# A gated recurrence over 512 steps: 24 sums of weights moved from GpSimd to VectorE

## The chip, the cores and the metric

The kernel runs on one core of one Trainium2 chip. The time is device time in microseconds. A core has five engines that run their own instruction queues in order and meet at semaphores: TensorE (PE; its weight loads are shown apart as PEld), VectorE (DVE), ScalarE (ACT), GpSimd (POOL) and SyncE (SP), which here only issues transfers between HBM and SBUF, the on-chip memory. Matmuls write to a second on-chip memory, PSUM.

## The reference

x is (8, 512, 512): 8 sequences, 512 steps, 512 features. One gated recurrent layer runs over the steps and its states are added to x:

```python
def step(h, x_t):
    fused = sigmoid(concatenate([x_t, h], -1) @ w_W + w_b)
    r, z = split(fused, 2, -1)
    m = x_t @ wx_W + wx_b + r * (h @ wh_W + wh_b)
    h_new = z * h + (1 - z) * tanh(m)
    return h_new, h_new
_, hs = scan(step, h0, swapaxes(x, 0, 1))
return x + swapaxes(hs, 0, 1)
```

All products with x_t (512 by 1536 weights) can be taken for many steps at once. The products with h (again 512 by 1536) can't: each step needs the state of the step before.

## The kernel before, in words

*Layout.* The 512 units stand in four blocks `k` of 128 partitions. A matmul takes 32 columns of the state or of x (4 steps of 8 sequences) as its stationary operand and writes 32 rows of PSUM. The steps are handled in groups of 4, and in chunks of `TC` = 16 steps, for which x is loaded and the output stored.

*One step of the recurrence.* TensorE takes the state's products in an order written out by hand (`ORDER`): A0 to A3 (parts of all gates, one for each block k), D0 to D3, and of H only the last two blocks. All of them are issued through the helper at L203. Behind them, in the same queue, stand a few matmuls of the x side, named xp by their output. VectorE then works in one chain: transposes of PSUM to the layout of the scans (tr and tz at L523, md1A at L538, md1B at L580), scans (L511) that give m, ScalarE's sigmoid and tanh in between (L243), and scans that give the new state hT. The state has two halves of two blocks each, and the second half (hd0B) comes last. A0 of the next step waits for the first scan of hT and A3 for the last.

*The end of a step.* Behind the last scan VectorE has `turn_x` (L282, a transpose for a later group), in some steps `drain` (L403), in steps 0 to 3 a quarter of `weight_sum(3)` (L296), and two memsets of one column (L654). Then comes the first transpose of the next step, tr, which waits for A on TensorE. GpSimd has at the end of each step the sum of x and the state, ot (L675), and behind it the list `jobs[i]` of the step.

*The x side.* The x products of the first two chunks are taken directly: `prefill`, 4 matmuls of 384 columns at a time. Each of them shows as two records, so one `take` shows as 8 records of xp. Step 0 takes 1, steps 1 and 2 three each, step 3 two, and steps 4 to 13 one or two each by `PLAIN`. From chunk 2 on, they go through a recursive scheme with fewer products in two levels (7 products in place of 8 at each level): `products` issues 3 or 4 small blocks a step from step 14 on, `x_sum` and `inner_x` form sums of x on GpSimd (so at L330, si at L349), `drain` collects on VectorE and `result` on GpSimd.

*The sums of weights.* The scheme needs sums of the weights wx, once. The outer level has four, `weight_sum` (tw, L296), on VectorE: three ahead of step 0 and the fourth in quarters in steps 0 to 3. The inner level has 24 instructions, `inner_weight(n, p)` (ti, L315): sum n of 4, for the part p of 6. Part 0 is 768 elements on each of 128 partitions, the others 384. Parts 0 and 2 read wx, parts 3 to 6 read tw 0 to 3. Sum 1 reads sum 0, and sum 3 reads sum 1. Before the change all 24 are on GpSimd: four ahead of step 0, three a step in steps 0 to 2, two in step 3, and one a step after that until step 12. The first product that reads ti is issued in step 16.

*What sets the order.* `tc.manual_schedule()` is on: every engine runs its instructions in the order in which the program issues them.

Of the kernel before, what the change touches and what calls it, by code (L numbers as in the profile page):

```python
# [10 lines left out]
ALU = mybir.AluOpType  # L11
# [43 lines left out]
def tile_cond_rnn_residual(  # L55
# [39 lines left out]
    nc = tc.nc  # L95
# [86 lines left out]
    ti = const.tile([P, 7, 4, NQ, BL], F32, name="ti")  # L182
# [101 lines left out]
    def wx_of(kh, nh):  # L284
        return wx[:, 2 * kh : 2 * kh + 2, :, HALF * nh : HALF * nh + HALF]

    def weight_sum(n, k=slice(0, 2), j=slice(0, NQ)):

        a, b = [
            (wx_of(0, 1), wx_of(0, 0)),  # L290
            (wx_of(1, 1), tw[:, 0]),
            (wx_of(1, 1), wx_of(0, 1)),
            (wx_of(1, 0), tw[:, 1]),
        ][n]
        at = (slice(0, P), k, j)
        nc.vector.tensor_tensor(tw[:, n][at], a[at], b[at], ALU.subtract)  # L296

    def inner_weight(n, p):

        def w(k, b):  # L300
            c0 = slice(BL * b, BL * b + BL)
            if p == 0:
                return wx[:, k::2, :, c0]
            if p == 2:
                return wx[:, 2 + k, :, HALF + BL * b : HALF + BL * b + BL]
            return tw[:, p - 3, k, :, c0]

        at = slice(0, 2) if p == 0 else p
        a, b = [
            (w(0, 1), w(0, 0)),  # L310
            (w(1, 1), ti[:, at, 0]),
            (w(1, 1), w(0, 1)),
            (w(1, 0), ti[:, at, 1]),
        ][n]
        nc.gpsimd.tensor_tensor(ti[:, at, n], a, b, ALU.subtract)  # L315

    def x_block(c, r, kh):

# [119 lines left out]
    for e in range(NQ):  # L438
        turn_x(0, e)
    weight_sum(1)  # L440
    for n in (0, 2):
        for p in (0, 2):
            inner_weight(n, p)

    jobs = {}

    def at_step(i, *todo):
        jobs.setdefault(i, []).extend(todo)

    early = [(1, 0), (1, 2)] + [(n, p) for n in (0, 2, 1) for p in (3, 4, 5)]  # L450
    for n, w in enumerate(early):
        at_step(n // 3, (inner_weight, *w))
    for n, w in enumerate([(0, 6), (1, 6), (2, 6), (3, 3), (3, 4), (3, 5), (3, 6), (3, 0), (3, 2)]):
        at_step(4 + n, (inner_weight, *w))
    drains = {}
    for c in range(2, NCH):
        w0 = TC * c - LEAD
# [3 lines left out]
        for w in range(TC):  # L461
            n = done
# [10 lines left out]
    for i in range(T):  # L473
# [176 lines left out]
            seed(5)  # L650
        if i < 4:
            weight_sum(3, *[slice(v, v + 1) if w == 0 else slice(2 * v, 2 * v + 2) for w, v in enumerate(divmod(i, 2))])
        for n in range(IDLE - 3):
            nc.vector.memset(idle[:, n : n + 1], 0.0)  # L654
        def add(hf, engine):
# [105 lines left out]
```

## Time and profile before

| | |
|---|---|
| median of 3 runs | 1645.9 us (1644.61 to 1647.66) |
| the profiled execution | 1646.05 us, span of its trace 1644.0 us |
| PE busy | 1628.2 us, 99% |
| DVE busy | 1379.4 us, 84% |
| ACT busy | 976.8 us, 59% |
| POOL busy | 569.3 us, 35% |
| TensorE clock granted | 1.0 |

Each row of a timeline gives the start in microseconds from the span's beginning, the duration, the engine, the line, the operation, what is written and read, and in brackets the idle time before it with what ended it. Several equal instructions in a row are merged ("x32"). A matmul's duration includes its way through the array, so that rows of TensorE overlap; the distance between two starts is what TensorE spends on the first. The chain that ended last is followed back from the end of the program, at each instruction to what released it.

### The profile page before, as it was taken

The page shows a single profiled execution, that of the slowest core. Times are in us where ns is not written, and L with a number is a line of the kernel's source. Part 1 is how long each engine was busy: PE and PEld are TensorE (multiplying, and loading weights), DVE is VectorE, ACT ScalarE, POOL GpSimd, SP SyncE. Part 2 cuts the span into 40 slices and gives each one's busy share as a digit, 9 for nine tenths or more (in the row PEclk, how much of TensorE's full clock was granted, in tenths as well). Part 3 has the DMA queues.
Part 4 walks back from the last instruction along what each step waited for, and adds up shares of the span by engine and source line. Part 5 has one row for each costly group of instructions (what it writes and reads, how often), then busy time and mean ns, then how long its engine had stood idle before and what let it go on. Part 6 is the DMA issues. An engine that isn't in the chain of part 4 may idle for free.

```text
span 1644.0 us, 124813 instructions
## 1 busy us (share of the span) xinstructions
PE 1628.2 (99%) x53006; PEld 1360.1 (83%) x53006; DVE 1379.4 (84%) x11215; ACT 976.8 (59%) x5520; POOL 569.3 (35%) x1467
## 2 busy tenths in 40 slices
PE   8999999999999999999999999999999999999998
PEld 4788888888888888888888888888888888888876
DVE  8688888888888888888888888888888888888886
ACT  3666656556555656666656656655655566666665
POOL 7433333333333333333333333333333333333220
PEclk9999999999999999999999999999999999999999
DMA  4000000000000000000000000000000000000000
GB/s 181 11 10 18 18 18 17 6 18 17 18 18 5 18 18 18 18 17 5 18 18 18 18 5 18 18 18 17 18 5 18 18 18 18 5 18 11 12 11 10
DMA packets 11512, 31.08 MB, mean 19 GB/s; under 512 B 1220, under 2 KB 1732, under 8 KB 10952
## 3 DMA queue, kind: packets, MB, share of 16 engines
q1 hardware_dynamic: 10800, 22.94, 4.1%
q8 instruction: 414, 6.78, 1.7%
q14 instruction: 146, 1.20, 0.2%
q10 hardware_dynamic: 152, 0.16, 0.0%
HBM read 14.70 MB, written 8.39 MB: 14 GB/s over the span
## 4 chain that ended last, share of the span: by engine, by line
PE 97%; DVE 2%; POOL 1%; DMA 0%; issue 0%; ACT 0%; DVEq 0%; POOLq 0%
PE A L203 48%; PE D L203 26%; PE xp L203 16%; PE H L203 7%; DVE tr L523 0%; DVE m L511 0%; POOL ti L315 0%; DMA rows<-in_bias_dram 0%; DVE hT L511 0%; POOL xs L225 0%; DVE md1B L580 0%; DVE md1A L538 0%; DVE tz L523 0%; POOL off L229 0%; DVE tw L296 0%
## 5 line engine op out<-in xcount | busy, mean ns | idle before, releaser
L203 PE MATMUL A<-wa,hT 128*32 128x256 f32 x16352 | 885.9, 356 | 5.7 <-DVE hT L511 5.2
L203 PEld LDWEIGHTS A<-wa,hT 128*32 128x32 f32 x16352 | 507.7, 123 | 241.4 <-DVE hT L511 138.9
L203 PE MATMUL D<-wd,hT 128*32 128x128 f32 x16384 | 543.1, 273 | 1.0 <-DMA wd<-in_wd_dram 1.0
L203 PEld LDWEIGHTS D<-wd,hT 128*32 128x32 f32 x16384 | 482.8, 122 | 21.7 <-DMA wd<-in_wd_dram 1.3
L675 POOL TENSOR_TENSOR ot<-xin,hT 128x32 f32<-128x32 f32 x503 | 132.3, 263 | 1047.3 <-DVE hT L511 1035.9
L243 ACT ACTIVATE hT<-m 128x8 f32<-128x8 f32 x2048 | 324.4, 207 | 98.0 <-DVE m L511 97.7
L243 ACT ACTIVATE md0A<-tr 128x16 f32<-128x16 f32 x512 | 112.9, 220 | 407.3 <-DVE tr L523 407.3
L523 DVE STREAM_TRANSPOSE tr<-A 128x64 f32<-128x64 f32 x511 | 127.7, 250 | 229.1 <-PE A L203 229.1
L243 ACT ACTIVATE hT<-hT 128x16 f32<-128x16 f32 x1024 | 233.1, 228 | 85.0 <-DVE hT L511 84.2
L203 PE MATMUL H<-wa,hT 128*32 128x64 f32 x8208 | 210.3, 219 | 0.0
L203 PEld LDWEIGHTS H<-wa,hT 128*32 128x32 f32 x8208 | 187.5, 122 | 0.0
L511 DVE TENSOR_TENSOR_SCAN hT<-hd0A,hT 128x24 f32<-128x24 f32 x1024 | 176.3, 172 | 0.0
L511 DVE TENSOR_TENSOR_SCAN hT<-hd0B,hT 128x24 f32<-128x24 f32 x1024 | 154.4, 192 | 21.8
L511 DVE TENSOR_TENSOR_SCAN m<-md0B,md1B 128x24 f32<-128x24 f32 x1024 | 154.5, 192 | 0.0
L203 PE MATMUL xp<-ti,si 128*32 128x96 f32 x5040 | 150.1, 246 | 0.2 <-issue 0.2
L511 DVE TENSOR_TENSOR_SCAN m<-md0A,md1A 128x16 f32<-128x16 f32 x1024 | 144.2, 182 | 5.1
L243 ACT ACTIVATE md0B<-tr 128x16 f32<-128x16 f32 x512 | 116.2, 227 | 42.2 <-DVE tr L523 0.5
L418 POOL TENSOR_TENSOR xs<-ff 128x192 f32<-128x192 f32 x240 | 140.6, 596 | 0.2
L580 DVE STREAM_TRANSPOSE md1B<-A 128x64 f32<-128x64 f32 x511 | 130.0, 254 | 0.0
L243 ACT ACTIVATE hd0A<-tz 128x16 f32<-128x16 f32 x512 | 116.6, 228 | 21.4
L538 DVE STREAM_TRANSPOSE md1B<-H 128x64 f32<-128x64 f32 x512 | 127.8, 250 | 0.0
L573 DVE STREAM_TRANSPOSE hd0B<-sz 128x64 f32<-128x64 f32 x512 | 126.4, 247 | 0.0
(103 smaller groups left out, 1924.4 us busy)
## 6 DMA issues: line engine op xcount, KB each, us to landing
xin<-in_x_dram SPq DMA_DIRECT2D x31, 256.0 KB, 3.3
out_dram<-ot SPq DMA_DIRECT2D x31, 256.0 KB, 2.2
wx<-in_wx_dram SPq DMA_DIRECT2D x4, 768.0 KB, 7.1
wa<-in_wa_dram SPq DMA_DIRECT2D x4, 512.0 KB, 9.7
wd<-in_wd_dram SPq DMA_DIRECT2D x1, 768.0 KB
wd<-in_wd_dram SPq DMA_DIRECT2D x1, 256.0 KB, 11.2
out_dram<-ot SPq DMA_DIRECT2D x1, 192.0 KB, 1.8
head<-in_xh_dram ACTq DMA_DIRECT2D x1, 144.0 KB, 5.1
```

The source lines that it names most:

```text
L203: nc.tensor.matmul(out_, lhsT, rhs, start=start, stop=False, skip_group_check=True)
L243: inst = nc.scalar.activation(out_, in_, func, **kw).ins
L418: nc.gpsimd.tensor_tensor(to, a, b, ALU.add)
L511: return nc.vector.tensor_tensor_scan(*[t_[:, :, c_].rearrange("p n c s -> p (n c s)") for t_ in (out_, d0, d1)], 0.0, ALU.mult, ALU.add,).ins
L523: inst = nc.vector.transpose(t_.rearrange("p c n -> p (c n)"), raw[n][hf]).ins
L538: inst = nc.vector.transpose(md1[hf][g % 2][:, :, :, hf].rearrange("p n c -> p c n"), raw["h"][hf]).ins
L573: inst = nc.vector.transpose(hd0[1][i % 2][:, :, :, 2].rearrange("p n c -> p c n"), sz).ins
L580: nc.vector.transpose(md1[1][g % 2][:, :, :, 0].rearrange("p n c -> p c n"), ps["A"][:, :HU])
L675: pool_done[i + 1] = nc.gpsimd.tensor_tensor(ot[:, t], x_of(c, slice(0, NQ), t, 1), hTs[(i + 1) % NH][:, :, :, B * s1 : B * s1 + B, 2].rea ...
```

## The change

`inner_weight` issues its subtraction on VectorE in place of GpSimd. Of the 24, sum 0 of the parts 0 and 2 stay ahead of step 0. The other 22 are listed in `late` and issued at the ends of steps 0 to 13, behind `weight_sum` and ahead of the two memsets: two digits are n and p, and "|" divides the steps. `late` is no part of `jobs`, so these sums stand in VectorE's queue ahead of the first transpose of the next step.

```diff
-        nc.gpsimd.tensor_tensor(ti[:, at, n], a, b, ALU.subtract)
+        nc.vector.tensor_tensor(ti[:, at, n], a, b, ALU.subtract)
...
     weight_sum(1)
-    for n in (0, 2):
-        for p in (0, 2):
-            inner_weight(n, p)
-
-    jobs = {}
+    for p in (0, 2):
+        inner_weight(0, p)
+
+    jobs, late = {}, {}
...
-    early = [(1, 0), (1, 2)] + [(n, p) for n in (0, 2, 1) for p in (3, 4, 5)]
-    for n, w in enumerate(early):
-        at_step(n // 3, (inner_weight, *w))
-    for n, w in enumerate([(0, 6), (1, 6), (2, 6), (3, 3), (3, 4), (3, 5), (3, 6), (3, 0), (3, 2)]):
-        at_step(4 + n, (inner_weight, *w))
+    for n, w in enumerate("03 04|05|23|24|25 13|14 15|06 26|16|10|12 22|20|30|32 33|34 35 36".split("|")):
+        late[n] = [tuple(map(int, v)) for v in w.split()]
...
             weight_sum(3, *[slice(v, v + 1) if w == 0 else slice(2 * v, 2 * v + 2) for w, v in enumerate(divmod(i, 2))])
+        for w in late.get(i, ()):
+            inner_weight(*w)
         for n in range(IDLE - 3):
             nc.vector.memset(idle[:, n : n + 1], 0.0)
```

## The prediction

> **What bounds the kernel now.** I read the page first, then the chain that ended last, cut to 15 to 40 us, and then the timelines of TensorE, VectorE and GpSimd up to 110 us.
>
> ```profile
> span 1644.0 us, 124813 instructions
> ...
> PE 1628.2 (99%) x53006; PEld 1360.1 (83%) x53006; DVE 1379.4 (84%) x11215; ACT 976.8 (59%) x5520; POOL 569.3 (35%) x1467
> ```
>
> A busy share of 99% says little where all stages are averaged. The change touches only the first 14 of 512 steps, so the timeline of TensorE over those steps is the view that counts. Columns: start, duration, engine, line, operation, and what ended the idle time before.
>
> ```profile
> 18.10 1.10 PE L203 MATMUL D<-wd,hT 128*32 128x128 f32 x32 [0.97 <-DMA wd<-in_wd_dram]
> 19.01 0.63 PE L203 MATMUL H<-wa,hT 128*32 128x64 f32 x32
> 19.46 0.83 PE L203 MATMUL xp<-wx,head 128*32 128x384 f32 x8
> ...
> 28.48 1.06 PE L203 MATMUL D<-wd,hT 128*32 128x128 f32 x32
> ...
> 33.03 1.06 PE L203 MATMUL D<-wd,hT 128*32 128x128 f32 x32
> ...
> 37.38 1.06 PE L203 MATMUL D<-wd,hT 128*32 128x128 f32 x32
> ...
> 41.27 1.06 PE L203 MATMUL D<-wd,hT 128*32 128x128 f32 x32
> 42.15 0.41 PE L203 MATMUL H<-wa,hT 128*32 128x64 f32 x16
> 42.37 0.83 PE L203 MATMUL xp<-wx,xin 128*32 128x384 f32 x8
> 43.02 1.70 PE L203 MATMUL A<-wa,hT 128*32 128x256 f32 x32
> 44.53 1.06 PE L203 MATMUL D<-wd,hT 128*32 128x128 f32 x32
> ...
> 66.64 1.06 PE L203 MATMUL D<-wd,hT 128*32 128x128 f32 x32
> ...
> 70.11 1.06 PE L203 MATMUL D<-wd,hT 128*32 128x128 f32 x32
> ...
> 74.01 1.06 PE L203 MATMUL D<-wd,hT 128*32 128x128 f32 x32
> ...
> 77.14 1.06 PE L203 MATMUL D<-wd,hT 128*32 128x128 f32 x32
> ```
>
> The rows D are one to a step, so I use their starts as the clock; D(i) is that of step i, D(0) at 18.10. From 41.27 to 44.53 (steps 5 and 6) TensorE starts each block when the one before has been issued: D 0.88, H 0.22, xp 0.65 for 8 records, A 1.51, together 3.26. So a step with 8 records of xp takes 3.25, one with 16 takes 3.90 (37.38 to 41.27, step 4), one with 24 takes 4.55 (28.48 to 33.03, step 2). These are TensorE's own times, which no other engine's relief can shorten. Three places are longer: up to 28.48; step 3 with 16 records (33.03 to 37.38, 4.35 in place of 3.90, 0.45 lost); step 12 with 8 records (66.64 to 70.11, 3.47 in place of 3.25, 0.22 lost). From step 14 on (74.01 to 77.14) a step takes 3.13, and this goes on to the end.
>
> What is lost in the first two places is told by the chain, and by VectorE's rows.
>
> ```profile
> 15.99 5.55 POOL ti L315 x4
> 22.15 0.20 DVE hT L511
> ...
> 22.99 0.22 DVE md1A L282
> 23.21 1.69 DVE tw L296
> ...
> 35.20 0.80 DVE hT L511
> 36.06 1.50 PE A L203 x24
> ```
>
> ```profile
> 13.48 1.71 DVE L296 TENSOR_TENSOR tw<-wx,tw 128x1536 f32<-128x1536 f32 x1
> 17.18 0.25 DVE L523 STREAM_TRANSPOSE tr<-xp 128x64 f32<-128x64 f32 x1 [1.99 <-PE xp L203]
> ...
> 17.71 1.10 DVE L511 TENSOR_TENSOR_SCAN m<-md0A,md1A 128x16 f32<-128x16 f32 x2
> 19.26 0.25 DVE L523 STREAM_TRANSPOSE tr<-D 128x64 f32<-128x64 f32 x1 [0.45 <-PE D L203]
> 19.43 1.20 DVE L511 TENSOR_TENSOR_SCAN hT<-hd0A,hT 128x24 f32<-128x24 f32 x1
> ...
> 20.70 0.90 DVE L511 TENSOR_TENSOR_SCAN hT<-hd0A,hT 128x24 f32<-128x24 f32 x1
> ...
> 36.76 0.52 DVE L296 TENSOR_TENSOR tw<-wx,tw 128x384 f32<-128x384 f32 x1
> ...
> 48.68 0.25 DVE L523 STREAM_TRANSPOSE tr<-A 128x64 f32<-128x64 f32 x1 [1.10 <-PE A L203]
> ...
> 49.56 0.24 DVE L523 STREAM_TRANSPOSE tr<-D 128x64 f32<-128x64 f32 x1
> 49.73 0.17 DVE L511 TENSOR_TENSOR_SCAN hT<-hd0A,hT 128x24 f32<-128x24 f32 x1
> ...
> 50.73 0.18 DVE L511 TENSOR_TENSOR_SCAN hT<-hd0B,hT 128x24 f32<-128x24 f32 x1
> ...
> 51.94 0.25 DVE L523 STREAM_TRANSPOSE tr<-A 128x64 f32<-128x64 f32 x1 [0.90 <-PE A L203]
> ```
>
> The scan that takes 0.17 at 49.73 takes 1.20 and 0.90 in step 0, while POOL's four sums of L315 run, and 0.80 in step 3; a tw of 384 takes 0.52 at 36.76, and 1.69 in the chain for the same size at 23.21. VectorE's two-input work and POOL's sums exclude each other here, an instruction at a time. Rows of POOL show it from the other side, and what POOL keeps:
>
> ```profile
> 36.81 0.59 POOL L675 TENSOR_TENSOR ot<-head,hT 128x32 f32<-128x32 f32 x1 [0.87 <-DVE hT L511]
> ...
> 45.13 0.47 POOL L330 TENSOR_TENSOR so<-xin 128x128 f32<-128x128 f32 x1
> ...
> 47.53 0.26 POOL L675 TENSOR_TENSOR ot<-head,hT 128x32 f32<-128x32 f32 x1 [1.51 <-DVE hT L511]
> ```
>
> The ot row takes 0.26 alone and 0.59 beside the tw of 36.76.
>
> **The change, part by part.** *Removed from POOL:* all its sums of L315, four ahead of step 0 (5.55) and the rest behind the ot of each step. POOL ends no step, so this alone is worth only what it stops holding up.
>
> *Step 0.* VectorE's tr of D still starts at 19.26, since D waits for a load until 18.10. In the undisturbed step 7 the last scan of hT starts 1.17 behind that transpose (49.56 to 50.73). H of step 0 has 32 records in place of 16, which puts it 0.22 later, so the last scan starts at about 20.65, not 22.15. TensorE then has work without a gap: H, xp of 8 records (19.46), A of step 1 at 20.11; its last quarter, which needs that scan, at 20.11 + 3/4 x 1.51 = 21.24. D(1) comes at 18.10 + 0.91 + 0.45 + 0.65 + 1.51 = 21.62.
>
> *Step 1.* VectorE has, behind the scan, 0.84 of waiting for ScalarE's copy (22.15 to 22.99), then tw and the two new sums of 384 (numbers 03 and 04). I price a sum of 384 at 0.52, the tw row of the same size, and one of 768 at 0.92, on the line between 0.52 and the 1.71 of 1536. That gives 20.65 + 0.84 + 0.22 (the chain's md1A) + 3 x 0.52 = 23.3 for the next tr. This is 1.4 later than TensorE could serve it, but the first scan of hT starts 1.05 behind tr (48.68 to 49.73) and the last ends 2.23 behind it (50.73 + 0.18), at 24.5 and 25.5. A(2) starts behind 24 records, at 21.62 + 4.55 - 1.51 = 24.66, and its last quarter, which reads the last scan's part, at 25.8. TensorE just misses waiting: D(2) = 26.17, not 28.48, **2.31 gained**. If the tr were 0.5 later, 0.2 to 0.3 of that would go.
>
> *Two sums ahead of step 0* (768 and 384, 1.44) fall into the 1.99 for which VectorE waits before 17.18. Were that cover gone, step 0 still has the 0.45 idle before 19.26 and the disturbed scans' 0.9 ahead of it.
>
> *Steps 1 to 13.* VectorE needs 2.36 of a step of its own (51.94 - 48.68 - 0.90). In steps 1 to 3 come tw and one sum: 3.40 against 4.55, 4.55, 3.90. Steps 4, 6, 9 have two sums: 3.40 against 3.90; steps 8 and 11 one of 768: 3.28 against 3.90. Steps 5 and 12 have two sums and step 10 one of 768: 3.40 and 3.28 against 3.25, up to 0.15 late, but each is followed by a step of 16 records, in which the scans have 3.90 - 3.13 = 0.77 to spare. So **0.45** (step 3) and **0.22** (step 12) come back. Step 13 has three sums: 2.36 + 1.56 = 3.92 against 3.90, and if POOL's ot of 0.26 gets in between, 4.18; behind it comes a step of 3.13 without room, so **0.2 is lost** there (between 0 and 0.3).
>
> *Waits and queues.* The sums wait for nothing that comes late, and stand ahead of the next step's first transpose in VectorE's queue, which is counted above. What waits for ti is TensorE at step 16, three steps behind the last sum. No DMA moves. TensorE will want the second half of x's first chunk at 22.7:
>
> ```profile
> 9.42 4.62 SPq L119 DMA_DIRECT2D xin<-in_x_dram  x4
> ...
> xin<-in_x_dram SPq DMA_DIRECT2D x1, 128.0 KB, 9.7
> ```
>
> It lands at 9.42 + 9.7 = 19.1, in time. POOL's ot and its so and si jobs (0.26 to 0.47) now start at the end of the same step and meet the new sums. Between the bounds, a sum of 384 costs from 0.52 (nothing in the way) to 0.52 + 0.47 = 0.99 (one POOL job ahead of each); below 0.52 no row goes. I take 0.52, since the ot of 36.81 was the one that waited, not tw. The Trainium skill, page "SBUF — State Buffer", section "Who interferes with whom", says that a VectorE instruction with two SBUF inputs contends with a GpSimd one that reads SBUF, that whoever issues first holds the pair for the whole instruction, and that the other fully blocks. By that rule alone POOL's jobs hold up the new sums as often as they are held up, and the sum would be that of the first rival below; the stretched rows above agree with the lock itself, and no row of before shows two sums in a row with POOL between.
>
> *Sum.* 2.31 + 0.45 + 0.22 - 0.2 = 2.8. The profiled execution took 1646.05, so it would take 1643.25; the median of the runs shown is 1645.9, 0.15 less, so I predict **1643.1**, 0.17% less.
>
> **The rivals.** *Slower: VectorE becomes the bound of steps 1 to 13.* TensorE's time for them is 2 x 4.55 + 7 x 3.90 + 4 x 3.25 = 49.4. VectorE's is 13 x 2.36 + 3 x 0.52 + 23 d, where d is the cost of a sum of 384 and 768 counts twice: 32.3 + 23 d. At 0.52 that is 44.2. It passes TensorE's at d = 0.74 and eats the whole gain of 2.98 at d = 0.87. With the upper bound 0.99 it is 55.0, 5.6 lost, 1646.05 - 2.98 + 5.6 = 1648.7, on the median 1648.5. For it: the lock shown above, and POOL jobs in steps 4 to 11. Against it: steps 1 to 3, 12 and 13 have only the ot. Chance 0.1, half of it beyond 0.2%.
>
> *Only the late stalls go.* If step 0 is held by something that stands behind POOL's sums and that no row shows, the last scan stays near 22.15, tw falls from 1.69 to 0.52 and the two sums take 1.04 of that back: D(2) gains 0.1, the others 0.67, less 0.2: 0.6, 1645.3. Against it: VectorE's scans in step 0 have no idle time before them that something else ended. Chance 0.1.
>
> *The other 498 steps shift.* Nothing of the change runs there, but 0.01 in each is 5 us, either way: 1638 or 1648. Chance 0.03 each.
>
> **How the numbers follow.** About 0.2%, 3.3 us, is what a measurement of this kernel can tell from no change; the three runs lie 3.05 apart. My case has 0.74. Its 2.8 lies 0.5 below that bound, so the measured difference may well pass it: 0.36 faster, 0.38 within. Its own range is 1642.0 to 1644.5. With the late-stall case the range is 1641.9 to 1645.5; outside remain most of the slower rival, the shifts and the edges of my own case, 2 in 10. Faster 0.36 + 0.03 = 0.39; slower 0.05 + 0.03 = 0.08, which I set to 0.10 for a collision priced too low; same 0.51.
>
> **What would show it.** Right: scans of step 0 at 0.2 and no L315 on POOL; D(2) near 26.2, D(4) near 34.6, D(14) near 71.2; steps of 3.13 afterwards. Wrong: rows of L315 on VectorE well above 0.52, idle time of VectorE before tr gone with TensorE waiting for hT in steps 4 to 13, or D(1) still near 23.

## The result and the profile after

The changed kernel takes 1643.83 us (median of 18 runs, 1641.65 to 1645.41), the kernel before 1646.83 beside it (18 runs, 1644.61 to 1649.39): ratio 0.9979, 95% interval 0.9972 to 0.9986, so faster by 0.21%, or 3.0 us between the medians. The prediction said 2.8 us less, 1643.1; that figure started from 1645.9, and the kernel before came out 0.9 higher in these runs, so the differences are what compares.

TensorE's timeline after the change, with the rows D as the clock of the steps, as in the prediction:

```profile
17.92 1.11 PE L203 MATMUL D<-wd,hT 128*32 128x128 f32 x32 [0.96 <-DMA wd<-in_wd_dram]
18.84 0.63 PE L203 MATMUL H<-wa,hT 128*32 128x64 f32 x32
19.29 0.83 PE L203 MATMUL xp<-wx,head 128*32 128x384 f32 x8
19.93 1.70 PE L203 MATMUL A<-wa,hT 128*32 128x256 f32 x32
21.45 1.06 PE L203 MATMUL D<-wd,hT 128*32 128x128 f32 x32
...
25.99 1.06 PE L203 MATMUL D<-wd,hT 128*32 128x128 f32 x32
...
34.44 1.06 PE L203 MATMUL D<-wd,hT 128*32 128x128 f32 x32
...
66.96 1.06 PE L203 MATMUL D<-wd,hT 128*32 128x128 f32 x32
...
70.86 1.06 PE L203 MATMUL D<-wd,hT 128*32 128x128 f32 x32
...
73.99 1.05 PE L203 MATMUL D<-wd,hT 128*32 128x128 f32 x32
```

From D(0), which still waits for its load, to D(14) there is no idle time on TensorE any more. Counted from each kernel's own D(0), so that a load that lands 0.18 earlier doesn't count, D(14) comes at 70.86 - 17.92 = 52.94 in place of 74.01 - 18.10 = 55.91: 2.97 us less, in the stage where the change is. Then a step takes 3.13, as before.

VectorE in the same stretch:

```profile
14.99 1.68 DVE L315 TENSOR_TENSOR ti<-wx 128x768 f32<-128x768 f32 x2
17.02 0.25 DVE L519 STREAM_TRANSPOSE tr<-xp 128x64 f32<-128x64 f32 x1 [0.35 <-PE xp L203]
...
17.55 0.28 DVE L507 TENSOR_TENSOR_SCAN m<-md0A,md1A 128x16 f32<-128x16 f32 x2
19.09 0.25 DVE L519 STREAM_TRANSPOSE tr<-D 128x64 f32<-128x64 f32 x1 [1.26 <-PE D L203]
19.27 0.17 DVE L507 TENSOR_TENSOR_SCAN hT<-hd0A,hT 128x24 f32<-128x24 f32 x1
...
20.56 0.18 DVE L507 TENSOR_TENSOR_SCAN hT<-hd0B,hT 128x24 f32<-128x24 f32 x1
...
21.55 0.51 DVE L296 TENSOR_TENSOR tw<-wx,tw 128x384 f32<-128x384 f32 x1
21.98 1.02 DVE L315 TENSOR_TENSOR ti<-tw 128x384 f32<-128x384 f32 x2
22.93 0.24 DVE L519 STREAM_TRANSPOSE tr<-A 128x64 f32<-128x64 f32 x1
...
37.02 0.51 DVE L315 TENSOR_TENSOR ti<-tw 128x384 f32<-128x384 f32 x1
37.46 0.62 DVE L315 TENSOR_TENSOR ti<-tw,ti 128x384 f32<-128x384 f32 x1
...
69.47 1.52 DVE L315 TENSOR_TENSOR ti<-tw,ti 128x384 f32<-128x384 f32 x3
...
71.11 0.25 DVE L519 STREAM_TRANSPOSE tr<-A 128x64 f32<-128x64 f32 x1
```

The scans of step 0 are at 0.17 where they had 1.20 and 0.90; the last one of the state starts at 20.56 in place of 22.15. The tw at the end of step 0 takes 0.51, not 1.77. Sums of 384 start 0.43 to 0.44 apart when one follows the other (21.55 to 21.98, 37.02 to 37.46).

GpSimd now waits in its turn. The same ot of 0.26 takes 0.58 to 0.99 beside the sums:

```profile
37.08 0.58 POOL L673 TENSOR_TENSOR ot<-head,hT 128x32 f32<-128x32 f32 x1 [3.40 <-DVE hT L507]
37.62 0.77 POOL L330 TENSOR_TENSOR so<-xin 128x128 f32<-128x128 f32 x1
...
51.31 0.99 POOL L673 TENSOR_TENSOR ot<-xin,hT 128x32 f32<-128x32 f32 x1 [1.96 <-DVE hT L507]
```

Nothing on the path waits for them.

The two profiled spans differ by 3.6 (1644.0 and 1640.4): 0.18 from the load, 2.97 up to D(14), and 0.45 behind it. That last part is no trend: at the first transpose of the steps 15, 128, 256, 384 and 480 the changed kernel is ahead by 3.15, 3.25, 3.94, 4.34 and 3.64.

### The profile page after: what moved, and what is told of

Read it like the earlier page. It is cut to its first block, busy times and chain, and to the rows that moved or that the text cites. A ratio compares the mean times of both kernels' runs of the same rounds, so it can differ in the third digit from the quotient of the medians.

```text
span 1640.4 us, 124811 instructions
## 1 busy us (share of the span) xinstructions
PE 1627.4 (99%) x53006; PEld 1362.0 (83%) x53006; DVE 1384.8 (84%) x11239; ACT 977.2 (60%) x5520; POOL 550.3 (34%) x1443
## 4 chain that ended last, share of the span: by engine, by line
PE 97%; DVE 1%; DMA 1%; issue 0%; SPq 0%; ACT 0%; DVEq 0%
PE A L203 48%; PE D L203 26%; PE xp L203 16%; PE H L203 7%; DMA wd<-in_wd_dram 1%; DVE tr L519 0%; DVE m L507 0%; DMA head<-in_xh_dram 0%; DVE md1B L576 0%; DVE md1A L534 0%; DVE tz L519 0%; DVE hT L507 0%; SPq L142 0%; ACT hT L243 0%; DVE idle L542 0%
## 5 line engine op out<-in xcount | busy, mean ns | idle before, releaser
L673 POOL TENSOR_TENSOR ot<-xin,hT 128x32 f32<-128x32 f32 x503 | 136.0, 270 | 1048.4 <-DVE hT L507 1036.9
L507 DVE TENSOR_TENSOR_SCAN hT<-hd0A,hT 128x24 f32<-128x24 f32 x1024 | 171.6, 168 | 0.0
```

Of the source, the lines that this page charges most:

```text
L507: return nc.vector.tensor_tensor_scan(*[t_[:, :, c_].rearrange("p n c s -> p (n c s)") for t_ in (out_, d0, d1)], 0.0, ALU.mult, ALU.add,).ins
L673: pool_done[i + 1] = nc.gpsimd.tensor_tensor(ot[:, t], x_of(c, slice(0, NQ), t, 1), hTs[(i + 1) % NH][:, :, :, B * s1 : B * s1 + B, 2].rea ...
```

## The experiments

Seven kernels. The clock of each is D(i) - D(0) of its own profile, in which steps that nothing disturbs agree to 0.02 us between kernels:

| kernel | D(1) | D(2) | D(4) | D(14) | D(17) | ratio to before (95%) |
|---|---|---|---|---|---|---|
| before | 4.88 | 10.38 | 19.28 | 55.91 | 65.34 | 1 |
| changed | 3.53 | 8.07 | 16.52 | 52.94 | 62.33 | 0.9979 (0.9972 to 0.9986) |
| memsets for sums | 3.81 | 8.36 | 16.80 | 53.22 | 62.64 | 0.9979 (0.9969 to 0.9988) |
| late on GpSimd | 3.79 | 8.33 | 16.78 | 58.80 | 68.82 | 1.0013 (1.0004 to 1.0023) |
| each sum twice | 3.53 | 9.08 | 17.52 | 59.19 | 72.53 | 1.0032 (1.0022 to 1.0043) |
| split at step 4 | 3.52 | 8.07 | 16.51 | 56.84 | 66.24 | one run |
| order kept, GpSimd | 4.08 | 8.62 | 17.07 | 58.79 | 68.18 | one run |
| spare sums in step 0 | 6.04 | 10.58 | 19.02 | 55.45 | 64.85 | one run |
| two memsets more | 3.52 | 8.07 | 16.51 | 52.93 | 62.33 | one run |

The four kernels with one run took 1648.09, 1652.24, 1648.68 and 1645.72 us, in the order of the table; beside the first, the kernel before has a median of 1647.78, beside the others single runs of 1653.84 (for two of them) and 1647.39. The 18 runs of the kernel before spread over 4.8 us, so a pair of single runs can't tell 3 us (by its one pair, the kernel with the order kept would be faster than before, by D(14) it is slower). These four are read by their rows and their D alone.

**Memsets for the sums.** On the kernel before:

```diff
-        nc.gpsimd.tensor_tensor(ti[:, at, n], a, b, ALU.subtract)
+        nc.gpsimd.memset(ti[:, at, n], 0.0)
```

> The kernel before, with each of the 24 sums of L315 replaced by a memset of the same part of ti, on GpSimd at the same place: the sums are left out, ti is zero. GpSimd has as many instructions as before, but they read nothing from SBUF. My theory: VectorE was held by GpSimd instructions that read SBUF, so the scans of step 0 fall to 0.2, D(2) - D(0) is 8.07 as in the changed kernel (before: 10.38) and D(14) - D(0) is 52.94 (before: 55.91), some 3 us faster than before. It is also the floor: no sum runs on VectorE, so if the sums on VectorE cost anything, this is below 52.94. Rival, GpSimd's queue being occupied at all (ot and what waits for it late) was what cost: D(14) - D(0) stays above 54, since memsets of this size occupy it for a good part of the time.

Rows of VectorE and of GpSimd in its step 0:

```profile
17.92 0.28 DVE L511 TENSOR_TENSOR_SCAN m<-md0A,md1A 128x16 f32<-128x16 f32 x2
...
20.68 0.21 DVE L511 TENSOR_TENSOR_SCAN m<-md0B,md1B 128x24 f32<-128x24 f32 x1 [0.24 <-issue]
```

```profile
16.14 2.13 POOL L315 MEMSET ti<- 128x768 f32 x4
```

Two scans run in 0.28, from 17.92 on, while GpSimd writes ti until 18.27. With sums in that place, the same two took 1.10. So it isn't GpSimd's work that held VectorE, but work that reads SBUF. A limit of the experiment: memsets are shorter (2.13 for the four, against 5.55) and are over before the scans of the state, so only the two scans of m show it in step 0. In step 1 VectorE's tw shows it again: it takes 0.52 (from 22.20) inside three memsets (21.68 to 23.14), where it took 1.77 beside sums. D(1) is 3.81, not the expected 3.53; from there on each step to D(14) agrees with the changed kernel to 0.01 or 0.02. The missing 0.28 lies in the idle time marked "issue"; the last experiment is about it.

**Late on GpSimd.** On the kernel before, place without engine:

```diff
-    for n in (0, 2):
-        for p in (0, 2):
-            inner_weight(n, p)
...
+    for n, w in enumerate("00 02|20 22|03 04|05 06|10 12|23 24|13 14|25 26|15 16|30 32|33 34|35 36".split("|")):
+        at_step(2 + n, *[(inner_weight, *map(int, v)) for v in w.split()])
```

> The kernel before with all 24 sums on GpSimd still, but none ahead of step 2: two at the end of each of steps 2 to 13. Tells place from engine. My theory: the 2.31 of steps 0 and 1 come back without VectorE (D(2) - D(0) = 8.07), and later two sums a step hold the scans of the next step in the short steps (8 records) for 0.3 to 0.8 each: D(14) - D(0) between 53.2 and 55. Rival, the engine is what counts: near 55.9 as before or above.

The first half held: D(4) is 16.78, the 0.28 apart as in the changed kernel, with all sums on GpSimd. The second half was wrong by far: D(14) is 58.80, and the kernel is slower than before. The sums cost it in steps of 16 records too. VectorE and GpSimd at the start of step 6, which takes 4.28 in place of 3.90:

```profile
44.19 1.33 DVE L504 TENSOR_TENSOR_SCAN m<-md0A,md1A 128x16 f32<-128x16 f32 x2
```

```profile
43.06 1.99 POOL L315 TENSOR_TENSOR ti<-tw 128x384 f32<-128x384 f32 x2
45.01 0.46 POOL L330 TENSOR_TENSOR so<-xin 128x128 f32<-128x128 f32 x1
```

One sum of 384 at the end of a step is over when the next step's scans begin; that is how the kernel before lost nothing in steps 4 to 11. Two aren't, and then the sums of x follow. The two scans, 0.28 when undisturbed, end at 45.52 behind them. I had priced this hold at 0.3 to 0.8 in short steps alone. A spread that keeps the sums on GpSimd at one a step can't place 24 between step 2 and the first product in step 16; whether another order there would cost less was not tried.

**Each sum twice.** On the changed kernel:

```diff
-        nc.vector.tensor_tensor(ti[:, at, n], a, b, ALU.subtract)
+        for _ in range(2):
+            nc.vector.tensor_tensor(ti[:, at, n], a, b, ALU.subtract)
```

> The changed kernel with each sum issued twice on VectorE (same result). My theory: a sum of 384 costs 0.43 there when one follows another, so VectorE passes TensorE's time in the steps with two sums and the kernel becomes bound by it: D(14) - D(0) about 59, between 57.5 and 59.5 (changed kernel: 52.94, before: 55.91), so slower than before by 1.5 to 3.5 us. Rival, the sums are hidden on VectorE whatever their number: 52.94.

D(14) is 59.19, as expected, but the time is 1652.74 against 1647.78 for before beside it, 5.0 more and not 1.5 to 3.5. Rows of VectorE and TensorE behind step 13 show what I left out:

```profile
76.38 3.23 DVE L316 TENSOR_TENSOR ti<-tw,ti 128x384 f32<-128x384 f32 x6
79.55 0.24 DVE L520 STREAM_TRANSPOSE tr<-A 128x64 f32<-128x64 f32 x1
```

```profile
80.81 2.31 PE L203 MATMUL A<-wa,hT 128*32 128x256 f32 x32 [2.03 <-DVE hT L508]
82.88 1.95 PE L203 MATMUL D<-wd,hT 128*32 128x128 f32 x32
84.59 0.67 PE L203 MATMUL H<-wa,hT 128*32 128x64 f32 x16
```

The six sums of step 13 reach TensorE only at A of step 15, so that D(14) is too early a mark; at D(17) the kernel is 7.19 behind the one before and 10.20 behind the changed one. Not all of that is VectorE's work. Behind the wait of 2.03 the clock granted to TensorE fell to 0.50, from about 82.0 to 85.3; before and behind that it is 1.00. A takes 2.07 up to the start of D in place of 1.54, D 1.71 in place of 0.88, and step 15 as a whole 4.31 in place of 3.13: with the 0.53 of A, 1.7 in all. That the wait brought the lower clock is not shown; the other kernels have waits of up to 1.31 in these steps, and none of them has a clock below 1.00 there.

Now the first rival of the prediction can be tried. Six sums in 3.23 are 0.54 each, 1.08 for a doubled one, and 32.3 + 23 x 1.08 = 57.1, 7.7 over TensorE's 49.4. The sum counts the sums at the ends of steps 1 to 13, which delay steps 2 to 14. Of the 10.20, 1.01 is step 1 (D(2) is 9.08 and not 8.07), 1.7 the lower clock, and the rest, 7.5, stands against the 7.7: VectorE is the bound there. Set against before, the 7.7 would be 4.8, once the 2.98 are taken off. That the medians say 5.0 (3.6 to 7.1 by the interval) is no proof of it, since the 4.8 leaves out step 1 and the clock. Single sums of 384, at 0.43 to 0.62, stay under the 0.74 at which VectorE's time passes TensorE's.

**Split at step 4.** On the changed kernel, the sums of steps 4 to 13 go back to GpSimd, spread over the same steps:

```diff
-    for n, w in enumerate("03 04|05|23|24|25 13|14 15|06 26|16|10|12 22|20|30|32 33|34 35 36".split("|")):
+    for n, w in enumerate("03 04|05|23|24".split("|")):
         late[n] = [tuple(map(int, v)) for v in w.split()]
+    for n, w in enumerate("25|13|14|15|06 26|16|10 12|22 20|30|32 33|34|35|36".replace(" ", "|").split("|")):
+        at_step(4 + n * 10 // 17, (inner_weight, *map(int, w), nc.gpsimd))
```

> The changed kernel up to step 3; the 17 sums from step 4 on are back on GpSimd, in nearly the same steps (4 to 13), behind ot and ahead of the sums of x. My theory: up to D(4) as in the changed kernel (16.52 behind D(0)); then two GpSimd sums of 1.0 hold the next step's scans, and steps with 8 records lose 0.2 to 1.0 each: D(14) - D(0) between 53.2 and 54.5. Rival, GpSimd does the late sums for nothing and only the first steps matter: 52.94.

Up to D(4) nothing differs (16.51). From there to D(14) it takes 40.33 in place of 36.42: 3.91 lost, more than the 0.3 to 1.6 expected. The worst step, 10 (8 records, 4.84 in place of 3.25), in rows of VectorE and of GpSimd:

```profile
58.73 2.02 DVE L509 TENSOR_TENSOR_SCAN m<-md0A,md1A 128x16 f32<-128x16 f32 x2
```

```profile
57.60 2.83 POOL L315 TENSOR_TENSOR ti<-wx 128x384 f32<-128x384 f32 x2
60.37 0.54 POOL L349 TENSOR_TENSOR si<-xin 128x64 f32<-128x64 f32 x2
```

The second scan gets its turn when the second sum, one of 768, is over at 60.43. With nearly the same sums at the same steps, at mostly two a step, the engine decides.

**Order kept, GpSimd.** The changed kernel with the first line of its diff undone, so that the sums run on GpSimd, in the new order (each step's ahead of its ot):

> The changed kernel's order with the sums back on GpSimd (the engine undone, the order kept, so that each step's sums stand ahead of its ot). My theory: step 0 is held as before, D(1) - D(0) about 4.9 (changed kernel 3.53), D(2) - D(0) 9.3 to 10.4, D(14) - D(0) 54.5 to 56.5. Rival, the order is what was gained: 53.

Rows of VectorE in its step 0:

```profile
17.47 1.11 DVE L507 TENSOR_TENSOR_SCAN m<-md0A,md1A 128x16 f32<-128x16 f32 x2
...
19.64 0.89 DVE L507 TENSOR_TENSOR_SCAN hT<-hd0A,hT 128x24 f32<-128x24 f32 x1
```

Step 0 is held, but D(1) is 4.08 and not 4.9: only four sums of 768, 384, 384, 384 stand ahead of its ot, and the last scans of the state get through behind them. D(2) (8.62) misses too: step 1 takes 4.54, as in the changed kernel, since a single sum stands behind that ot where the kernel before has three. D(14) is 58.79, above the 54.5 to 56.5 expected. The order alone gains 1.76 up to D(2), by the later place of the sums, and has lost 2.88 against before by D(14).

**Spare sums in step 0.** The changed kernel with GpSimd doing four sums that nobody reads, and nothing else changed:

```diff
         inner_weight(0, p)
+    spare = const.tile([P, 2, NQ, BL], F32, name="spare")
+    for _ in range(2):
+        nc.gpsimd.tensor_tensor(spare, wx[:, 0::2, :, BL : 2 * BL], wx[:, 0::2, :, :BL], ALU.subtract)
+        nc.gpsimd.tensor_tensor(spare[:, 0], wx[:, 2, :, HALF + BL :], wx[:, 2, :, HALF : HALF + BL], ALU.subtract)
```

> The changed kernel with four sums into a spare tile on GpSimd ahead of step 0, of the sizes of the four that were there before, and nobody reading them. My theory: step 0 alone is held again, D(1) - D(0) = 4.9, last scan of the state near 22, D(14) - D(0) between 54.0 and 55.2 (changed kernel 52.94), and steps from 2 on as in the changed kernel. Rival, the step-0 sums on GpSimd were covered: 52.94.

Rows of VectorE and of GpSimd in its step 0:

```profile
17.79 1.67 DVE L511 TENSOR_TENSOR_SCAN m<-md0A,md1A 128x16 f32<-128x16 f32 x2
...
20.54 1.82 DVE L511 TENSOR_TENSOR_SCAN hT<-hd0A,hT 128x24 f32<-128x24 f32 x1
```

```profile
17.48 1.85 POOL L445 TENSOR_TENSOR spare<-wx 128x768 f32<-128x768 f32 x1
19.40 1.00 POOL L446 TENSOR_TENSOR spare<-wx 128x384 f32<-128x384 f32 x1
20.49 1.82 POOL L445 TENSOR_TENSOR spare<-wx 128x768 f32<-128x768 f32 x1
```

The hold is back in step 0, and larger than in the kernel before: D(1) 6.04 against 4.88, since the spare sums start at 17.48 and not at 15.95 and so lie on the scans with their whole length. The scan of 20.54 lasts until the sum beside it ends. Every later step is as in the changed kernel: D(14) - D(1) is 49.41 in both. Four sums on GpSimd in step 0 cost 2.51 here, alone.

**Two memsets more.** The kernel with memsets for the sums, and on VectorE, ahead of step 0:

```diff
     weight_sum(1)
+    for n in range(2):
+        nc.vector.memset(idle[:, n : n + 1], 0.0)
```

> The kernel with memsets on GpSimd in place of the sums (the sums left out, ti is zero), with two memsets of one column put on VectorE ahead of step 0, where the changed kernel has its two sums. That kernel and the one with the late sums on GpSimd had D(1) - D(0) = 3.81 and 3.79, against 3.53 in the changed one, and between two scans of step 0 an idle time of 0.22 to 0.24 put down to issue. If the idle time hangs on how many instructions VectorE has behind it (its instructions arriving), it goes or moves with two more: D(1) - D(0) = 3.53. If it hangs on VectorE not having worked just before step 0, two instructions of 0.06 change nothing: 3.8.

A row of VectorE in its step 0:

```profile
19.79 0.31 DVE L513 TENSOR_TENSOR_SCAN m<-md0B,md1B 128x24 f32<-128x24 f32 x2
```

The two scans that stood 0.45 apart now run in 0.31, D(1) is 3.52, and the rest follows. No sum runs on VectorE in this kernel, and D(14) is 52.93; in the changed one, with 24 sums there, it is 52.94. So up to D(14) the sums on VectorE cost nothing.

## Why the prediction was right

*Step 0 and 1, 2.31.* Right. D(1) was to come 3.52 behind D(0) and does at 3.53, D(2) 8.07 and does at 8.07. The last scan starts 2.64 behind D(0), where 2.55 was worked out. Of the 2.31, 1.35 is step 0 (4.88 against 3.53) and 0.96 step 1 (5.50 against 4.54). For step 0, the memsets show that reads by GpSimd held it, and the spare sums that such a hold in step 0 alone costs this much and more (2.51, with the sums lying later). For step 1, rows of the kernel before show VectorE's quarter of tw beside two sums of GpSimd (the first is of 768, and one of 768 takes 1.85 elsewhere, so by this estimate it ends near 24.5, and tw, which takes 0.51 alone, ends at 24.90):

```profile
23.13 1.77 DVE L296 TENSOR_TENSOR tw<-wx,tw 128x384 f32<-128x384 f32 x1
```

```profile
22.63 3.15 POOL L315 TENSOR_TENSOR ti<-wx,ti 128x768 f32<-128x768 f32 x2
```

Beside memsets that tw takes 0.52, and the kernels with memsets and with the late sums, which have no GpSimd sum there, take 4.55 and 4.54 for step 1. The number has luck in it: with a VectorE queue two instructions shorter, 0.28 of it would have gone to the idle time marked "issue", which the prediction knew nothing of. (The 24.5 that it gives for the start of the first scan of step 1 is that scan's end; 23.3 + 1.05 is 24.35. Nothing else hangs on it.)

*The sums' price, 0.52.* A little high: 0.43 from one start to the next, 0.92 for 768 as priced (51.26 to 52.18 in step 8 of the changed kernel). The tr behind the sums of step 0 came 5.01 behind D(0) and not 5.2, so that TensorE's last quarter of A had more to spare. The two sums ahead of step 0 took 1.68 in place of 1.44, beside a copy of GpSimd's, and left 0.35 of the 1.99 that covered them.

*Steps 3 and 12, 0.45 and 0.22.* Right: step 3 takes 3.90 and step 12 3.26 in the changed kernel. The prediction named no cause for step 12. In the kernel before, GpSimd's sum of step 11, one of 768, ends at 67.41, the sums si behind it run until 68.03, and the scans of step 12 wait among them:

```profile
67.42 0.66 DVE L511 TENSOR_TENSOR_SCAN m<-md0A,md1A 128x16 f32<-128x16 f32 x2
```

*Step 13, 0.2 lost.* Wrong, and the one term of the sum that was mis-sized: 0.00. The prediction had 2.36 + 1.56 + 0.26 = 4.18 for a step of 3.90. The three sums take 1.52 with GpSimd's ot among them: they start 0.43 apart and not 0.52, and an ot between two sums lengthens the second by 0.1 (0.62 for 0.51), not by its 0.26. So 2.36 + 1.52 = 3.88 just fits, and the tr at 71.11 stands 0.25 behind D(14) as ever. With that term at nothing the sum of the prediction is 2.98, against 2.97 in the trace.

*The rule on the shared pair of the Trainium skill* (page "SBUF — State Buffer", section "Who interferes with whom") has the mechanism: two-input VectorE work and GpSimd reads hold each other up, memsets on GpSimd don't (scans of 0.28 beside 2.13 of memsets). The prediction's reading of it, that GpSimd would hold up the new sums as often as it is held up, came true in number and not in price: in 9 of the steps 1 to 13 an ot got in between two of VectorE's sums, or tw and a sum, and ot went from 0.26 to 0.58 and more, a sum only from 0.51 to 0.62. The ot ends 0.13 behind the first sum (37.66 against 37.53), so once its turn came it had little left to do, and the second sum waited about as long.

*The rivals.* VectorE as the bound was real but needed sums of twice the price; there steps 2 to 14 lose 7.5 to it, where 7.7 is worked out. That only the late stalls go is refuted by D(1). A shift of the 498 other steps isn't seen: 3.13 before and after. The prediction gave its largest chance, 0.51, to a difference under the 3.3 us that it took for the least one can tell; 3.0 is under that, and 18 runs of each kernel tell it from nothing.

What stays open: the difference of the two profiled spans behind step 14 (0.45) is within what two executions of one kernel differ by (4.8 between the fastest and the slowest of 18), and wasn't pursued.

## What to carry to other kernels

An engine that ends no step can still hold the one that does, through a path that no semaphore shows: look for the same instruction at several durations (a scan at 0.17, 0.90 and 1.20) and for what runs beside the long ones. Moving such work to the held engine pays when its step has idle time waiting for a third engine, here 0.8 to 1.5 us a step from step 5 on, behind TensorE's x products. Before moving work only in time, check where its end falls: one GpSimd sum of 384 in a step's idle time cost nothing, two reached into the next scans and made the kernel slower than before.

## What the runs showed of the hardware that was not expected

Two short memsets on VectorE ahead of step 0 (0.07 us together) took away an idle time of 0.24 between two scans 5 us later, and 0.28 of the kernel's stage. The profile puts that idle time down to issue; that it hangs on where instructions stand in VectorE's stream is what the run suggests, the cause itself is not shown.

In these rows, what a hold costs depends on what the other side still has to do when it gets its turn: beside a GpSimd sum of 768 a scan lasts until the sum ends (1.82 for 0.17 at 20.54), while an ot of 32 elements between two VectorE sums delays the second by 0.1.

And in the kernel with doubled sums, behind a wait of 2.03, TensorE's granted clock fell to 0.50 for some 3.3 us, beginning about 1.2 us after TensorE had work again. It cost about 1.7, on top of the wait itself.
